# First transfers issued ahead of a branch, and one expert part's results added by matmuls instead of a store and a gather

## The chip, the core and the metric

The kernel runs on one core of a Trainium2 chip. The metric is the device time of one execution in microseconds (us); for the kernel before, the median of three runs is 1523.92 us, the lowest 1513.31 and the highest 1536.73. The core has engines that each work through an own queue in order: PE (TensorE, matmuls; its weight loads are listed apart as PEld), DVE (VectorE), ACT (ScalarE), POOL (GpSimd) and SP (SyncE, which here only issues transfers). Sixteen DMA engines carry the transfers that SP and POOL issue. Matmul results land in PSUM, everything else works in SBUF.

## The reference

The input x is 16 sequences of 256 tokens with 128 channels, 4096 tokens in all. Six sublayers follow each other, all with a residual:

```python
x = x + 0.5 * L0_ffn(layernorm(x))
x = x + L0_attn(layernorm(x))
x = x + 0.5 * L0_ffn(layernorm(x))
x = x + 0.5 * L1_ffn(layernorm(x))
x = x + L1_attn(layernorm(x))
x = x + 0.5 * L1_ffn(layernorm(x))
```

The attentions have 16 heads of 8 channels (layer 0 is the difference of two softmaxes, then a layernorm; layer 1 is causal with an output projection). Each feed-forward (FFN) is a mixture of eight experts of which each token uses two. For layer 1:

```python
gate_probs = softmax(xt @ Wg + bg)
top_v, top_i = top_k(gate_probs, 2)
w = top_v / (sum(top_v) + 1e-6)
a, g = split(xt @ W1[e] + b1[e]); act = a * gelu(g)
out = sum over the two experts of w * (act @ W2[e] + b2[e])
```

So a token's result is a weighted sum of two rows, one from each of its two experts. Layer 0 is alike with SwiGLU, 128 hidden channels in place of 256, no renormalised weights and one shared expert that every token uses.

## The kernel before, in words

**Blocks and parts.** The 4096 tokens are eight blocks of 512; all eight stay in SBUF as `xs[0..7]`. The first FFN treats blocks 0 and 1 densely (`dense`: all nine experts on the block, each expert's hidden rows multiplied by that expert's gate weight). The gate weights of a dense block are transposed into `cwT`, stored to DRAM (`cwD`) and loaded back as eight broadcast tiles `cwb` (line 897), each needed by one multiply on DVE.

All other FFN work is sparse and cut in parts of two blocks (`Sparse`, 16 parts); the last part of the last FFN is split into two parts of one block each: index 14 (block 6) and index 15 (block 7). A part goes through these tasks:

- `dispatch`: layernorm, gate logits, top two, and for each token and each of its two choices j the row (`idx`) it gets in a list of slots that is sorted by expert, each expert padded to a multiple of 128; and the two weights `wgt`, already halved.
- `scatter`: one indirect DMA per chunk of 128 tokens and per choice writes the normalised rows to `slots_x` in DRAM. The slots were zeroed by `clear_slots`.
- `load_tiles` and `compute`: for each tile of 128 slots the expert's weights are loaded from `wcat` (all weights and biases of an expert side by side, prepared in DRAM by `gather_weights`), and the rows from `slots_x`. A part of two blocks has 23 tiles, a part of one block 15. Two tiles at a time are transposed, multiplied, activated and multiplied again; the result y plus bias is stored to `slots_y`.
- `combine` and `add_to_x`: when all tiles of the part are stored, one indirect DMA per chunk and choice gathers the rows back (16 for a part of two blocks, 8 for one), and DVE adds each, times its weight, to x. The block's x is then final, and in the last FFN it is stored to the output.

**Order.** Nothing is ordered by hand. All tasks are generators that ask for an engine (`Ask`); a planner (`Tasks.run`) keeps a clock for each engine (`Clocks`, `Timed`: modelled durations) and gives the turn to the request with the smallest planned start plus 0.0048 us per rank (`HASTE`). Ranks are numbers by hand (`FFN_RANK`, `ATT_RANK`). The order so found is written into the engines' queues and is fixed on the chip. The planner books a DMA with 0.45 us on SP and its bytes at 300 GB/s behind the bytes ahead (`bytes_free`); a bulk transfer asks with `after=max(0.0, clocks.bytes_free - 3.0)`, not before the queue of bytes is shorter than 3 us. The indirect DMAs also wait for a matmul that the planner sees 1 us ahead of them ("pace", line 975).

**Branch.** A short calculation (`bound`, line 676) decides whether the scores of the attentions can overflow. Its result is read into a register (line 1306), and everything after is planned twice, once for each side of a branch. What is added to the planner ahead of line 1305 is planned and issued ahead of the branch: the loads that the first dense block needs, dense block 0, the normalised rows of blocks 0 and 1, and `bound`. `program` (line 1611) adds the rest, on each side: the clears, `gather_weights`, `dense(1)`, `loads(1)` (small constants and `xs[2..7]`), all sparse parts and attentions.

**Buffers** that the change touches: `big`, three PSUM tiles of 128x1024 (an FFN tile pair takes one for its hidden rows, an attention unit two); `b_s`, four SBUF tiles of 128x512; `b_y`, three; `b_cw`, two pairs of gate weight tiles for the dense blocks.

Of the kernel before, what the change touches and what calls it, by code (L numbers as in the profile page):

```python
# [9 lines left out]
FP = mybir.dt.float32  # L10
# [8 lines left out]
P = 128  # L19
# [10 lines left out]
HASTE = 0.0048  # L30

FFN_RANK = [
    [28, 13, 59],
    [190, 217, 235, 244],
    [218, 230, 258, 302],
    [450, 460, 412, 513, 477],
]
ATT_RANK = [
    [70, 127, 102, 103, 126, 127, 221, 222],
    [261, 262, 308, 271, 338, 301, 220, 513],  # L40
]


# [210 lines left out]
def kernel(ctx: ExitStack, tc: tile.TileContext, a: dict, out: bass.AP):  # L254
# [81 lines left out]
    def tile_of(shape, name, dtype=FP):  # L336
        return sb.tile(shape, dtype, name=name)
# [30 lines left out]
    )  # L368
    b_xn = buffers(5, [P, NCH, C], "xn")
    b_xnT = buffers(5, [P, TB], "xnT")  # L370
    b_cw = Buffers([(tile_of([P, NCH, E + 1], f"cw{i}"), tile_of([E + 1, TB], f"cwT{i}")) for i in range(2)])
    b_spread = buffers(3, [P, TB], "cwb")
    b_s = buffers(4, [P, TB], "s")
    b_h = buffers(3, [P, TB], "h")
# [114 lines left out]
    def loads(part):  # L489

        early = []
        for n in ("wq1", "wk1", "wq2", "wk2"):
            early.append((heads[n], a["L0_attn_" + n].rearrange("h c d -> c h d")))
        early += [(w1s[n], a["L1_attn_" + n]) for n in ("Wq", "Wk", "Wv")]
        early.append((heads["wv"], a["L0_attn_wv"].rearrange("h c d -> c h d")))
        early += [(xs[n], x_flat[n]) for n in range(2, PB)]
        late = [
            (sb2, a["L0_ffn_sb2"][0].partition_broadcast(P)),
            (gamma, a["L0_attn_ln_gamma"].partition_broadcast(P)),
            (beta, a["L0_attn_ln_beta"].partition_broadcast(P)),  # L500
            (lamb, a["L0_attn_lamb"].partition_broadcast(P)),
            (gate_w[1], a["L1_ffn_Wg"]),
            (gate_b[1], a["L1_ffn_bg"].partition_broadcast(P)),
            (w1s["Wo"], a["L1_attn_Wo"]),
            (b1_1raw, a["L1_ffn_b1"].rearrange("e (k f) -> (e k) f", f=P)),
        ]
        late += [(xs[n], x_flat[n]) for n in range(max(2, PB), NBLK)]
        for dst, src in early if part == 0 else late:
            yield Ask("SP")
            fetch(dst, src)  # L510

    def derived(part):
        if part == 0:
            yield from hidden_bias(b1_raw, b1_0)

            yield Ask("DVE", when=lambda: clocks.missing(b1_0) == 1)
            b = b1_0.rearrange("p (e k) -> p k e", k=2)[:, 0]
            nc.vector.tensor_scalar(b, b, 0.5, None, ALU.mult)
            return
        yield Ask("DVE", after=clocks.free["SP"] + 32.0)  # L520
        yield Ask("DVE", when=lambda: clocks.missing(sb2) == 1)
        nc.vector.tensor_scalar(sb2, sb2, 0.5, None, ALU.mult)

        yield Ask("DVE", after=clocks.free["SP"] + 60.0)
        yield vec(lamb, when=lambda: clocks.missing(gamma) == clocks.missing(beta) == 1)
        nc.vector.tensor_scalar(keep, lamb, -1.0, 1.0, ALU.mult, ALU.add)
        nc.vector.tensor_scalar(gamma, gamma, keep, None, ALU.mult)
        nc.vector.tensor_scalar(beta, beta, keep, None, ALU.mult)
        yield from hidden_bias(b1_1raw, b1_1)
# [10 lines left out]
    def clear_slots(h):  # L540
        v = slots_x[h].rearrange("(p i) d -> p i d", p=P)
        n = NSLOT // P
        step = -(-n // CLEAR)
        assert n > (CLEAR - 1) * step
        for i in range(0, n, step):
            m = min(step, n - i)
            yield Ask("SP", after=max(0.0, clocks.bytes_free - 3.0))
            nc.sync.dma_start(out=v[:, i : i + m, :], in_=zero.to_broadcast([P, m, C]))
# [10 lines left out]

    for layer in range(2):  # L560
        clocks.expect(wcat[layer], E // 4 + KF[layer] + 2)

    def gather_weights(layer, b1t, *deps):
        w1, w2, b2 = srcs[layer]
# [61 lines left out]
        number, pattern=[[1, NTILE], [0, E]], base=0, channel_multiplier=0,  # L626
        allow_small_or_imprecise_dtypes=True,
    )

    own4 = tile_of([P, 4, G], "own4")  # L630
    bare.gpsimd.memset(own4, 1.0)
# [239 lines left out]
    def dense_gates(run, rank):  # L871
        _, (tmp, gates, (cw, cwT)) = yield pe(
            run["xnT"], take=[(b_tmp, 1), (b_part, 1), (b_cw, 1)]
        )
        lg, taken = (t[:, :NCH] for t in gates)
        yield from gate_logits(run["xnT"], 0, lg)
        yield from choose(lg, taken)
        ex, mx = tmp[2][:, :NCH], tmp[6][:, :NCH].unsqueeze(2)
        yield from shares(lg, ex, mx)
        nc.vector.tensor_tensor(cw[:, :, 0:E], ex, taken, ALU.mult)  # L880
        nc.vector.memset(cw[:, :, E : E + 1], 1.0)
        b_tmp.put(tmp)
        b_part.put(gates)
        for i in range(BPB):
            _, (t,) = yield pe(cw, take=[(half, 1)])
            for c in range(NT):
                nc.tensor.transpose(t[: E + 1, c * P : (c + 1) * P], cw[:, i * NT + c, :], ident)
            yield from move(cwT[:, i * T : (i + 1) * T], t[: E + 1])
            half.put(t)
        run["cw"] = (cw, cwT)  # L890

        cwD = dram.tile([E + 1, TB], FP, name=f"cwD{run['n']}")
        yield Ask("SP", (cwT,))
        nc.sync.dma_start(out=cwD, in_=cwT)
        for e in range(E):
            _, (cwb,) = yield Ask("SP", (cwD,), take=[(b_spread, 1)])
            nc.sync.dma_start(out=cwb, in_=cwD[e : e + 1, :].to_broadcast([P, TB]))
            run["cwb"][e] = cwb

    def dense_expert(run, e):  # L900
# [31 lines left out]
            return  # L932
        nc.tensor.matmul(acc, lhsT=b2_0, rhs=run["cw"][1], start=False, stop=True)

        b_cw.put(run["cw"])
        b_xnT.put(xnT)
        _, (oT,) = yield Ask("ACT", (acc,), take=[(b_s, 1)])
        nc.scalar.copy(oT, acc)
# [41 lines left out]
    class Sparse:  # L980
        def __init__(self, index, layer, which, blocks, slots, rank, last=False):
            self.layer, self.last, self.rank = layer, last, rank
            self.after = 3 * layer + 2 * which
            self.blocks = blocks
            self.nch = len(blocks) * NCH
            self.ntile = 2 * self.nch + E - 1
            self.sx, self.sy = slots_x[slots], slots_y[slots]
            self.rows = rows_of[index]
            self.idx, self.wgt = (t[index][:, :, : self.nch] for t in (idx_of, wgt_of))
            self.gated = self.out_tiles = self.stored = 0  # L990
            self.scattered, self.weighed = [], False
            self.ready = False
            self.left = [NCH * 2 + (BPB if layer == 0 else 0) for _ in self.blocks]

        def add(self):
            tasks.add(self.rank - 5, self.dispatch())
            tasks.add(self.rank + 1, self.load_tiles())
            tasks.add(self.rank - 4, self.combine())

        def gate_block(self, i, xn, lg, taken):  # L1000
            n = self.blocks[i]
# [12 lines left out]
        def dispatch(self):  # L1014
# [96 lines left out]
            self.weighed = True  # L1111
            b_tmp.put(tmp)
            b_part.put(gates)

        def scatter(self, xns):
            def one(c, j):
                def issue(_):
                    row = xns[c // NCH][:, c % NCH, :]
                    s = bare.gpsimd.indirect_dma_start(  # L1119
                        out=self.sx[:, :],  # L1120
                        out_offset=bass.IndirectOffsetOnAxis(ap=self.idx[:, j, c : c + 1], axis=0),
                        in_=row, in_offset=None,
                    )
                    for t in self.scattered:
                        tc.declare_no_dep(s.ins, t.ins, reason="no slot twice")
                    self.scattered.append(s)
                    return s, [row, self.idx], self.sx

                return issue, (self.idx,)

            for i in range(len(xns)):
                todo = [one(c, j) for c in range(i * NCH, (i + 1) * NCH) for j in range(2)]
                yield from transfers(todo, lambda: not clocks.missing(self.sx))
                b_xn.put(xns[i])

        def shared(self, i, xnT):
            x = xs[self.blocks[i]]
# [67 lines left out]
        def compute(self, j, wts, xg, i0, last):  # L1205
# [53 lines left out]
                )  # L1259
            half.put(t)  # L1260
            b_wt.put(*wts)

            self.out_tiles += n
            late = 3.0 if self.out_tiles < self.ntile else 0.0
# [3 lines left out]
            )  # L1268
            b_y.put(y)
            self.stored += n  # L1270

        def combine(self):

# [22 lines left out]


    tasks.add(1, loads(0))
    tasks.add(0, derived(0))
    tasks.add(5, constants())  # L1300
    tasks.add(3, bound())
    for n in range(PB):
# [306 lines left out]
            bare.vector.tensor_copy(dst, m32.rearrange("p b t -> p (b t)"))  # L1609

    def program(shifted):
        for part in range(NPART):
            tasks.add(30 * (part + 3) % (30 * NPART), clear_slots(part))
        tasks.add(1, gather_weights(0, b1_0[:, 2 : 2 + 2 * E], b1_0))
        tasks.add(200, gather_weights(1, b1_1, b1_1))
        for n in range(1, PB):
            tasks.add(10 + n, dense(n, 10 + n))
        tasks.add(0, loads(1))
        tasks.add(3, derived(1))
        i = 0  # L1620
        for layer in range(2):
# [94 lines left out]
```

## Time and profile before

The profile is that of one execution, taken by the hardware profiler.

| what | value |
|---|---|
| median of three runs | 1523.92 us |
| the profiled execution | 1530.02 us |
| its span, first to last instruction | 1528.2 us |
| PE busy | 1244.2 us, 81% of the span |
| DVE busy | 933.3 us, 61% |
| ACT busy | 810.9 us, 53% |
| POOL busy | 621.2 us, 41% |
| mean granted PE clock | 0.904 of full speed |
| DMA | 232.87 MB, 152 GB/s on average |

How to read it: in the timeline a row is start, length, engine, source line, operation, tile written <- tile read, count; in brackets the idle time of the engine just before it, and what ended it. Nearly all instructions go through a helper at line 136, so the tile names tell them apart. "SPq" is SP's queue issuing a transfer; the data land later. The names are stripped of buffer numbers. The tiles `rw` and `cwb` are reused after the dense blocks: as `rw` also expert weights of sparse tiles are loaded, as `cwb` also rows of `slots_x`. A matmul of two 4-byte operands shows as two records.

### The profile page before, as it was taken

What the parts mean: (1) busy time and instruction counts of PE and PEld (TensorE: products, weight loads), DVE (VectorE), ACT (ScalarE), POOL (GpSimd) and SP (SyncE); (2) the same over time, 40 slices, a digit from 0 to 9 for tenths busy, and PEclk for the clock granted to TensorE, in tenths of its full rate; (3) what the DMA queues carried; (4) which work ended last, traced back from release to release, by engine and by line L of the source; (5) the groups of instructions that cost most, each with busy time, mean ns of one, the idle gap of its engine ahead of it and who ended that gap; (6) DMA issues with size and microseconds to landing.
All of it is one profiled execution on the core that took longest, in us unless ns stands there. A gap on an engine that the chain in (4) does not pass through costs nothing. (4 is left out here: it accounts for less than half of the span.)

```text
span 1528.2 us, 29302 instructions
## 1 busy us (share of the span) xinstructions
PE 1244.2 (81%) x9730; PEld 844.2 (55%) x9730; DVE 933.3 (61%) x3254; ACT 810.9 (53%) x1715; POOL 621.2 (41%) x629
## 2 busy tenths in 40 slices
PE   5848987888998988988987877788879789877872
PEld 3424554654444554545755665567468556656762
DVE  4464775855555545657666666878666664665543
ACT  2213555666776756656764564455546556653421
POOL 2013235344004044054264266653662564556233
PEclk8866999999999999899998999989789889988987
DMA  5185466651003435213756755565158542648893
GB/s 116 55 201 154 142 179 191 186 168 36 3 3 103 126 102 152 79 57 125 220 176 193 234 157 159 150 207 168 62 194 291 180 134 93 199 147 294 264 289 105
DMA packets 207531, 232.87 MB, mean 152 GB/s; under 512 B 32061, under 2 KB 151544, under 8 KB 207370
## 3 DMA queue, kind: packets, MB, share of 16 engines
q1 hardware_dynamic: 192010, 199.42, 42.9%
q0 software_dynamic: 15360, 31.49, 6.3%
q8 instruction: 79, 1.29, 0.4%
q14 instruction: 82, 0.67, 0.1%
HBM read 183.84 MB, written 52.75 MB: 155 GB/s over the span
## 5 line engine op out<-in xcount | busy, mean ns | idle before, releaser
L136 ACT ACTIVATE ex<-big 128x1024 f32<-128x1024 f32 (+1 forms) x384 | 350.2, 960 | 88.9 <-PE big L136 64.7
L1119 POOL DMA_INDIRECT slots_x<-xn,idx x240 | 242.0, 1008 | 270.3 <-PE big L136 86.9
L1278 POOL DMA_INDIRECT g<-slots_y,idx x240 | 236.4, 985 | 214.4 <-PE bank L136 94.9
L136 PE MATMUL big<-q,k 32*128 32x512 f32 (+1 forms) x1536 | 252.7, 639 | 14.6 <-ACT ex L136 5.8
L136 PE MATMUL big<-xT,wt 128*128 128x128 f32 x1456 | 222.4, 300 | 20.2 <-ACT xT L136 9.3
L136 PEld LDWEIGHTS big<-xT,wt 128*128 128x128 f32 x1456 | 203.1, 214 | 35.9 <-ACT xT L136 17.2
L136 PE MATMUL bank<-ex,vaug 128*32 128x256 f32 (+1 forms) x3072 | 189.4, 378 | 18.7 <-issue 6.3
L136 POOL TENSOR_TENSOR rstd<-rstd,mhalf 128x4 f32<-128x4 f32 (+1 forms) x64 | 62.1, 971 | 326.9 <-DVE rstd L136 325.8
L136 ACT ACTIVATE s<-big,wt 128x128 f32<-128x128 f32 x472 | 141.1, 377 | 87.9 <-PE big L136 54.4
L136 PEld LDWEIGHTS bank<-ex,vaug 128*32 128x32 f32 x3072 | 93.3, 113 | 92.0 <-issue 29.0
L136 PE MATMUL bank<-wt,h 128*128 128x128 f32 x728 | 118.6, 296 | 19.4 <-issue 7.8
L136 DVE SCALAR_TENSOR_TENSOR h<-big,wt,s 128x128 f32<-128x128 f32 x364 | 107.4, 343 | 41.4 <-ACT s L136 39.6
L136 PEld LDWEIGHTS big<-q,k 32*128 32x128 f32 x1536 | 82.6, 194 | 83.6 <-issue 50.0
L136 PEld LDWEIGHTS bank<-wt,h 128*128 128x128 f32 x728 | 99.5, 202 | 50.0 <-issue 20.2
L136 DVE SCALAR_TENSOR_TENSOR x<-g,wgt,x 128x128 f32<-128x128 f32 x240 | 88.5, 373 | 56.0 <-DMA g<-slots_y,idx 37.4
L136 PE MATMUL big<-xT,rw 128*128 128x128 f32 x716 | 113.2, 292 | 10.4 <-ACT s L136 3.7
L136 DVE TENSOR_TENSOR y<-bank,wt 128x128 f32<-128x128 f32 x236 | 59.8, 283 | 98.1 <-PE bank L136 34.3
L136 ACT COPY xT<-bank 128x256 f32<-128x256 f32 x180 | 61.4, 375 | 101.8 <-PE bank L136 63.2
L136 ACT COPY avs<-bank 128x256 f32<-128x256 f32 x96 | 36.1, 376 | 144.3 <-PE bank L136 71.8
L136 POOL TENSOR_TENSOR ex<-ex,causal 128x512 f32<-128x512 f32 x58 | 73.8, 1295 | 87.5 <-ACT ex L136 86.9
L136 PEld LDWEIGHTS big<-xT,rw 128*128 128x128 f32 x716 | 98.2, 204 | 19.1 <-issue 5.7
L136 ACT ACTIVATE s<-big,rw 128x128 f32<-128x128 f32 x232 | 72.1, 382 | 45.1 <-PE big L136 19.5
(192 smaller groups left out, 1835.2 us busy)
## 6 DMA issues: line engine op xcount, KB each, us to landing
wt<-wcat SPq DMA_DIRECT2D x128, 450.0 KB
rw<-wcat SPq DMA_DIRECT2D x63, 450.0 KB
wt<-wcat SPq DMA_DIRECT2D x108, 257.0 KB
slots_y<-y SPq DMA_DIRECT2D x168, 128.0 KB
rw<-wcat SPq DMA_DIRECT2D x53, 257.0 KB
cwb<-slots_x SPq DMA_DIRECT2D x45, 256.0 KB
xg<-slots_x SPq DMA_DIRECT2D x31, 256.0 KB
slots_x<-zero SPq DMA_DIRECT2D x12, 384.0 KB
```

Source lines behind the costliest of these rows:

```text
L136: r = f(*args, **kw)
L1119: s = bare.gpsimd.indirect_dma_start(out=self.sx[:, :], out_offset=bass.IndirectOffsetOnAxis(ap=self.idx[:, j, c : c + 1], axis=0), in_=ro ...
L1278: s = bare.gpsimd.indirect_dma_start(out=g[:, :], out_offset=None, in_=self.sy[:, :], in_offset=bass.IndirectOffsetOnAxis(ap=self.idx[:, j ...
```

## The change

Three things are changed.

1. *Ahead of the branch.* `loads(1)`, `gather_weights(0, ...)` and the clears of all four slot buffers are added to the planner ahead of line 1305 instead of in `program`. The loads of part 1 ask like other bulk transfers (`bytes_free - 3.0`). The two fixed delays in `derived(1)`: the first (32 us after SP's planned time) is 5 us.
2. *Part 14 is folded.* For this part, y is not stored and gathered. Each of its 8 pairs of chunk and choice writes for every token the pair (token number within the block, weight) to its slot in a small DRAM list `slots_t`, zeroed before; the list is loaded into SBUF as `told`, slot by partition. For each tile of 128 slots DVE builds a 128x512 matrix w (slot by token) that has the weight where the slot's token is, and zero elsewhere; four matmuls with w as the stationary operand add y's rows into an accumulator of 512 tokens in PSUM, held in one of the three `big` tiles from the first to the last tile of the part. Then one add on DVE brings it into x. The row of token numbers (`token`) takes the place of the gate weight tile of a dense block, so that tile has 128 partitions now.
3. *Ranks.* Ranks of some parts and attentions have other numbers.

The diff, cut:

```diff
 FFN_RANK = [
-    [28, 13, 59],
+    [33, 13, 59],
     [190, 217, 235, 244],
-    [218, 230, 258, 302],
-    [450, 460, 412, 513, 477],
+    [218, 230, 258, 222],
+    [450, 462, 417, 513, 466],
 ]
 ATT_RANK = [
-    [70, 127, 102, 103, 126, 127, 221, 222],
-    [261, 262, 308, 271, 338, 301, 220, 513],
+    [70, 125, 102, 103, 126, 127, 221, 222],
+    [261, 262, 295, 273, 340, 303, 270, 512],
 ]
...
         for dst, src in early if part == 0 else late:
-            yield Ask("SP")
+            yield Ask("SP", after=max(0.0, clocks.bytes_free - 3.0) if part else 0.0)
             fetch(dst, src)
...
-        yield Ask("DVE", after=clocks.free["SP"] + 32.0)
+        yield Ask("DVE", after=clocks.free["SP"] + 5.0)
...
+            self.fold = index == 14
+            self.acc, self.told, self.added = None, [], 0
...
+            if self.fold:
+                tasks.add(-10, clear_told())
+                self.left = [1]
+            else:
+                tasks.add(self.rank - 4, self.combine())
...
+            if self.fold:
+                nc.vector.tensor_copy(telling[:, :, :, 1], wgt)
+                yield from self.tell()
...
+        def tell(self):
+            yield Ask("POOL", writes=(token,))
+            nc.gpsimd.iota(token, pattern=[[1, TB]], base=0, channel_multiplier=0, ...)
...
+                    s = bare.gpsimd.indirect_dma_start(
+                        out=slots_t[:, :],
+                        out_offset=bass.IndirectOffsetOnAxis(ap=self.idx[:, j, c : c + 1], axis=0),
+                        in_=telling[:, j, c, :], in_offset=None,
+                    )
...
+            yield from transfers([one(c, j) for c in range(NCH) for j in range(2)])
+            yield Ask("SP", (slots_t,))
+            ld = nc.sync.dma_start(out=told, in_=slots_t.rearrange("(i p) k -> p i k", p=P))
...
+            if self.fold:
+                yield from self.fold_in(j, n, y)
+                return
...
+        def fold_in(self, j, n, y):
+            for i in range(n):
+                _, (w,) = yield Ask(
+                    "DVE", (told,), take=[(b_s, 1)], when=lambda: len(self.told) == 2 * NCH
+                )
+                nc.vector.tensor_scalar(
+                    w, token, told[:, j + i, 0:1], told[:, j + i, 1:2], ALU.is_equal, ALU.mult
+                )
...
+                acc = self.acc[:, 0, :]
+                yield pe(w, y, writes=[acc])
+                for c in range(NCH):
+                    nc.tensor.matmul(
+                        acc[:, c * P : (c + 1) * P], lhsT=w[:, c * P : (c + 1) * P],
+                        rhs=y[:, i, :], start=(self.added == c == 0),
+                        stop=(self.added == self.ntile - 1 and c == NCH - 1),
+                    )
+                self.added += 1
+                b_s.put(w)
+            b_y.put(y)
+            if self.added == self.ntile:
+                x = xs[self.blocks[0]].rearrange("p c d -> p (c d)")
+                yield vec(acc)
+                nc.vector.tensor_tensor(x, acc, x, ALU.add)
+                big.put(self.acc)
+                self.part_done(0)
...
+    tasks.add(2, loads(1))
+    tasks.add(11, gather_weights(0, b1_0[:, 2 : 2 + 2 * E], b1_0))
+    for part in range(NPART):
+        tasks.add(12 + 30 * (part + 3) % (30 * NPART), clear_slots(part))
...
     def program(shifted):
-        for part in range(NPART):
-            tasks.add(30 * (part + 3) % (30 * NPART), clear_slots(part))
-        tasks.add(1, gather_weights(0, b1_0[:, 2 : 2 + 2 * E], b1_0))
         tasks.add(200, gather_weights(1, b1_1, b1_1))
         for n in range(1, PB):
             tasks.add(10 + n, dense(n, 10 + n))
-        tasks.add(0, loads(1))
         tasks.add(3, derived(1))
```

More of the change, by code (lines that the diff above doesn't have):

```diff
@@ L370 @@
     b_xnT = buffers(5, [P, TB], "xnT")
-    b_cw = Buffers([(tile_of([P, NCH, E + 1], f"cw{i}"), tile_of([E + 1, TB], f"cwT{i}")) for i in range(2)])
+    b_cw = Buffers([(tile_of([P, NCH, E + 1], f"cw{i}"), tile_of([P, TB], f"cwT{i}")) for i in range(2)])
+    token = b_cw.free[1][1]
     b_spread = buffers(3, [P, TB], "cwb")
@@ L561, with clear_told @@
         clocks.expect(wcat[layer], E // 4 + KF[layer] + 2)
+    def clear_told():
+        yield Ask("SP")
+        nc.sync.dma_start(
+            out=slots_t.rearrange("(p i) k -> p (i k)", p=P),
+            in_=zero[:, 0, : 2 * NTOLD],
+        )
     def gather_weights(layer, b1t, *deps):
@@ L628 @@
     )
+    telling = tile_of([P, 2, NCH, 2], "telling")
+    bare.gpsimd.iota(
+        telling[:, :, :, 0], pattern=[[0, 2], [P, NCH]], base=0, channel_multiplier=1,
+        allow_small_or_imprecise_dtypes=True,
+    )
+    NTOLD = 2 * NCH + E - 1
+    slots_t = dram.tile([NTOLD * P, 2], FP, name="slots_t")
+    told = tile_of([P, NTOLD, 2], "tile_told")
     own4 = tile_of([P, 4, G], "own4")
@@ L874, in dense_gates @@
         )
+        run["bufs"] = (cw, cwT)
+        cwT = cwT[: E + 1]
         lg, taken = (t[:, :NCH] for t in gates)
@@ L933, in dense_expert @@
         nc.tensor.matmul(acc, lhsT=b2_0, rhs=run["cw"][1], start=False, stop=True)
-        b_cw.put(run["cw"])
+        b_cw.put(run["bufs"])
         b_xnT.put(xnT)
@@ L997, in add @@
             tasks.add(self.rank + 1, self.load_tiles())
-            tasks.add(self.rank - 4, self.combine())
+            if self.fold:
[3 more added lines that the diff above has]
+                tasks.add(self.rank - 4, self.combine())
         def gate_block(self, i, xn, lg, taken):
@@ L1134, in scatter, with one, issue @@
                 b_xn.put(xns[i])
+        def tell(self):
+            yield Ask("POOL", writes=(token,))
+            nc.gpsimd.iota(
+                token, pattern=[[1, TB]], base=0, channel_multiplier=0,
+                allow_small_or_imprecise_dtypes=True,
+            )
+            def one(c, j):
+                def issue(_):
+                    s = bare.gpsimd.indirect_dma_start(
[3 more added lines that the diff above has]
+                    )
+                    for t in self.told:
+                        tc.declare_no_dep(s.ins, t.ins, reason="no slot twice")
+                    self.told.append(s)
+                    return s, [telling, self.idx], slots_t
+                return issue, (telling, self.idx)
+            yield from transfers([one(c, j) for c in range(NCH) for j in range(2)])
+            yield Ask("SP", (slots_t,))
+            ld = nc.sync.dma_start(out=told, in_=slots_t.rearrange("(i p) k -> p i k", p=P))
+            for s in self.told:
+                tc.add_manual_dep(ld.ins, s.ins.name, SYNC, reason="every slot may be here")
         def shared(self, i, xnT):
@@ L1270, in compute @@
             self.stored += n
+        def fold_in(self, j, n, y):
+            for i in range(n):
+                _, (w,) = yield Ask(
+                    "DVE", (told,), take=[(b_s, 1)], when=lambda: len(self.told) == 2 * NCH
+                )
+                nc.vector.tensor_scalar(
+                    w, token, told[:, j + i, 0:1], told[:, j + i, 1:2], ALU.is_equal, ALU.mult
+                )
+                if self.acc is None:
+                    yield pe(w, y, when=lambda: self.acc is not None or big.free)
+                if self.acc is None:
+                    self.acc = big.free.pop()
+                acc = self.acc[:, 0, :]
[5 more added lines that the diff above has]
+                        stop=(self.added == self.ntile - 1 and c == NCH - 1),
+                    )
+                self.added += 1
[7 more added lines that the diff above has]
+                self.part_done(0)
         def combine(self):
```

## The prediction

> **What bounds the kernel now.** First the page's slices of the span, to find where TensorE (PE) is not filled; a digit is a tenth of a slice of 38.2 us, PEclk the granted clock.
>
> ```profile
> PE   5848987888998988988987877788879789877872
> PEclk8866999999999999899998999989789889988987
> DMA  5185466651003435213756755565158542648893
> ```
>
> The middle is full of PE work. Two places are not: slices 3 and 4 (76 to 153 us: clock at 0.6, DMA at 0.8), and the end, where DMA is at 0.8 to 0.9 for four slices and the last slice has almost no PE. The view of busy time by stretches prices both; columns are length, then PE, PE weight loads, DVE, ACT, POOL busy, then clock, DMA share, GB/s.
>
> ```profile
> 50.00:60.00 10.00, 8.74 (x32) 4.72 (x31) 7.95 (x13) 4.58 (x9) 0.00 (x0) 1.00 0.09 26
> 69.00:140.00 71.00, 43.05 (x126) 23.62 (x126) 38.48 (x137) 16.10 (x32) 8.07 (x8) 0.58 0.69 188
> 90.00:100.00 10.00, 0.00 (x0) 0.00 (x0) 9.41 (x38) 1.49 (x3) 1.42 (x2) 0.50 1.01 219
> 140.00:165.00 25.00, 23.42 (x131) 10.80 (x132) 16.31 (x53) 12.49 (x20) 15.07 (x16) 1.00 0.56 162
> 1405.00:1504.00 99.00, 75.54 (x563) 70.85 (x561) 48.00 (x197) 34.73 (x113) 30.23 (x32) 0.90 0.84 265
> ```
>
> Before the branch (it falls at 68.9 us) DMA is idle; after it 71 us hold only 43.05 x 0.58 = 25 us of full-clock PE work. The timeline shows what waits there.
>
> ```profile
> 68.92 3.26 SPq L136 DMA_DIRECT2D slots_x<-zero  x4
> 77.58 5.20 SPq L136 DMA_DIRECT2D x<-in_L_attn_x_dram  x6
> 84.03 0.29 DVE L136 BATCH_NORM_STATS2 st<-x 128x6 f32<-128x128 f32 x1 [6.26 <-DMA x<-in_L_attn_x_dram]
> 93.33 5.37 SPq L136 DMA_DIRECT2D wcat<-b_0t  x1
> 100.69 0.69 PE L136 MATMUL bank<-ident,xn 128*128 128x128 f32 x2 [16.09 <-DVE q L136]
> 112.12 0.31 SPq L136 DMA_DIRECT2D cwD<-cwT  x1
> 132.00 0.69 DVE L136 TENSOR_TENSOR h<-h,cwb 128x512 f32<-128x512 f32 x1
> ```
>
> DVE, in order, stands 6.26 us at the statistics of an x block that is fetched late; its held-up work then keeps PE idle for 16.09 us, and the second dense block's weights (cwb) are multiplied in only at 132. Last, the end:
>
> ```profile
> 1500.46 0.95 POOL L1278 DMA_INDIRECT g<-slots_y,idx  x1 [28.24 <-PE bank L136]
> 1502.93 0.61 PE L136 MATMUL bank<-rw,h 128*128 128x128 f32 x4
> 1503.58 0.29 DVE L136 TENSOR_TENSOR y<-bank,rw 128x128 f32<-128x128 f32 x1
> 1512.72 10.36 SPq L136 DMA_DIRECT2D out_dram<-x  x2
> 1519.85 0.95 POOL L1278 DMA_INDIRECT g<-slots_y,idx  x1 [0.30 <-issue]
> 1522.33 0.35 DVE L136 SCALAR_TENSOR_TENSOR x<-g,wgt,x 128x128 f32<-128x128 f32 x1 [0.90 <-DMA g<-slots_y,idx]
> ```
>
> PE is done at 1503.5, and 24.7 us follow to the span's 1528.2: sixteen gathers, one per 1.25 us on POOL (0.95 and 0.30 of issue), eight for each of the two one-block parts, then the last add and a store of 5.5 us. The first part's eight adds end with the first output at 1512.72.
>
> [...] 0.50 granted around the 16 us gap, 1.00 once PE is filled. [...] the two gathers timed cleanly in the chain take 2.24 and 2.41 us. [...] the trace's copy of b1_0t, 8 KB in 2048 pieces, held SP 5.37 us.
>
> **Part 1, transfers ahead of the branch.** Moved are 35 SP issues: 14 loads (8 small ones, 6 x blocks of 256 KB), 5 of the layer-0 weight gather (2 MB), 16 clears (5.9 MB), 9.4 MB in all. After the branch they took SP and DMA from 68.9 to about 115. From 20 to 69 us DMA was busy 12, 41, 8, 9 and 1% by tens, so there are some 42 us of room. Worth of it: the 71 us stretch. By PE alone, filled as in 140 to 165 (0.94), its 25 us would take 27: a gain of 44, the upper end. By DVE, 38.48 us of work: at 0.65 as in that next stretch 59 us (gain 12), at 0.94 as in 90 to 100 us 41 us (gain 30), at the middle, 0.80, 48 us (gain 23). I take **25**, a little over the middle, since some of that DVE work can move behind the stretch. The rest of the kernel is a chain of PE-filled stages and moves up with it. What is late next is DVE, then the second block's cwb.
>
> The cost is ahead of the branch. SP's queue is moved past by the cwD store and eight cwb loads of the first dense block (issued 28.0 to 51.8); the planner lets 3 us of bytes stand ahead of a bulk transfer, so a cwb can come 3 to 10 us late, the upper end with the 5.37 us of the b1_0t copy. Behind cwb wait DVE's multiply, then all behind it on DVE, then PE; the branch waits for them. DVE had a wait of 10.7 us at 44.9, where some of it hides. I take **+3**, range 0 to 10. No POOL instruction moves; POOL's first scatter (134.1) waits for clears that now end earlier.
>
> **Part 2, the fold of part 14.** Removed: 8 stores of y (15 tiles of 64 KB, 0.96 MB: 3.6 us at 265 GB/s), 8 gathers (10 us of POOL), 8 DVE adds (0.373 each, 3.0). Added on DVE: 15 weight builds 128x512, for which no row stands; 0.38 (the two-scalar row at 128x128) to 0.75 (the 128x512 row), taken 0.7: 10.5 us, hidden as DVE is at 48% from 1405 on, and as the weights can be built ahead of y. On PE: 4 matmuls a tile, recorded as 8 of about 0.112 us (16 took 1.79): 0.9 a tile, 13.4 in all, where PE is busy 75.5 of 99 us and DMA (0.84) sets the pace: most go into the 23 idle us. If that cover is gone, all 13.4 are on the path; none if DMA stays the bound; I take **+3**. On POOL: an iota (about 1 us by the 128x64 and 128x184 rows, 0.23 and 0.43) and 8 little scatters at 1.25: 11 us, beside a queue that idled 28 us before the end; the other part's gathers could slip by that. On SP: a clear and a load of 1920 pieces of 8 bytes, 0.5 to 5 us once, against 3.6 us of store issues saved: zero. DMA is relieved by 3.6; taken **-3**.
>
> The tail: last y at 1503.87, fold 1.1, add of acc to x 0.75, waits 0.3, store 5.5: 1511.5, that is -16.7. The other part's eight gathers, if still begun at 1500.46, end the kernel at 1512.7 + 5.5 = 1518.2: -10. With its rank lowered from 477 to 466 its tiles come a little sooner; I take **-14**.
>
> **Part 3, the ranks.** A rank counts 0.0048 us of planned start, so 80 ranks are 0.4 us: they reorder, not shift. Zero, with 8 us either way for another order. The shorter waits of the derived constants: zero.
>
> **Sum** against the profiled execution (1530.0; span 1528.2 and 1.8 around it): -25 +3 +3 -3 -14 = -36, so 1494. That execution stands 6.1 over the median of the runs shown (1523.9), so for the median 1488, 2.4% less.
>
> **Rivals.**
> *The lead is given back.* The stretch after the branch could be a latency chain (gate, choose, cwT, cwD, cwb), and the lead could run into a later stage that DMA sets. For it: from 100 to 120 us PE answers ACT and DVE piece by piece. Against: DVE's 6.26 us stand at a transfer, and the middle is PE-filled with DMA at 0 to 0.5 from slice 10 to 17. Front gain 5, tail 10: about 1509.
> *Slower, by PSUM.* The accumulator holds one of the three big tiles from its first fold to the end. From 1405 to 1504 there are 46 y adds, some 27 pairs of tiles, one per 3.7 us; with two tiles left, a pair may hold its tile 7.4 us. The trace shows 4.5 (1476.84 to 1481.35), but 10.8 in a stall (1453.54 to 1464.3). At 12 us held a pair takes 6: 27 x 2.3 = +62; less a tail of 14 and a front of 13 makes +35, 1559. It decides from about 11.5 us held.
> *It does nothing.* The moved transfers stand in SP's queue behind cwb loads that wait for DVE, and are issued at 50 to 69 us, little sooner than now; the fold's gathers are replaced by the other part's. About 1522.
>
> **Numbers.** Main case 0.80, its own range 1466 (DVE at 0.94, -30; no cost ahead; tail -17, relief -3; run scatter of 10) to 1503 (gain 12, cost 3, tail -10 and +3, -3; less scatter); 0.68 of it lies over 2% below the median (under 1493.4). Given back 0.06, nothing 0.03, slower 0.11. A change of about 2% is what a measurement of this kernel can tell from none. Faster 0.68, same 0.21, slower 0.11; the range 1464 to 1518 leaves out the slower case and a little at each end.
>
> **What would show it.** Right: x loads issued before the branch; no DVE wait for x; PE busy over 55 of the first 71 us after the branch at a clock over 0.8; the branch within 72 us; at the end eight gathers under the last matmuls and 8 to 15 us from the last matmul to the end. Wrong: DVE waiting for cwb before the branch for over 10 us; idle PE gaps after it that end with DVE as now; after 1400, PE waiting for a big tile to be freed, or a last stage longer by the whole 13 us.

## The result, and the profile after

The changed kernel takes 1504.44 us at the median of 10 runs (1493.35 to 1509.55), the kernel before 1522.66 of 10 on the same chip: a ratio of 0.988, 95% interval [0.9853, 0.9908], so 18.2 us or 1.2% less. The profiled execution took 1503.24 us (span 1501.5) against 1530.02; that pair differs by 26.8, since the profiled run of before was a long one. Four of the runs further down lie over 1.5% above the fastest of their kernel: the medians as given include them, the ratios and the differences between kernels in us leave them out.

The slices of the span of the changed kernel (37.5 us each):

```profile
PE   5768888899999898988987878778788888887886
PEclk8678999999999999899998999999998999989889
DMA  7545566730002443213656655455566255648974
```

The third slice of PE is 6 in place of 4, and the last 6 in place of 2; DMA is now at work in the second. But the second slice has a clock of 6, before 8, and PE of 7, before 8. The timelines show why. First of the kernel before:

```profile
26.54 0.30 SPq L136 DMA_DIRECT2D cwD<-cwT  x1
...
28.02 23.79 SPq L136 DMA_DIRECT2D cwb<-cwD  x8
...
32.33 1.89 DVE L136 TENSOR_TENSOR h<-h,cwb 128x512 f32<-128x512 f32 x3
...
58.96 0.69 DVE L136 TENSOR_TENSOR h<-h,cwb 128x512 f32<-128x512 f32 x1
...
68.08 0.16 DVE L136 TENSOR_SCALAR bounded<-bank 128x1 int32<-128x1 f32 x1 [0.68 <-PE bank L136]
```

Then of the changed kernel (`bounded` is the result of `bound`):

```profile
22.73 4.57 SPq L136 DMA_DIRECT2D x<-in_L_attn_x_dram  x5
27.41 0.36 SPq L136 DMA_DIRECT2D cwD<-cwT  x1
...
29.02 3.94 SPq L136 DMA_DIRECT2D slots_x<-zero  x3
...
34.67 1.54 SPq L136 DMA_DIRECT2D cwb<-cwD  x3
...
49.26 0.29 DVE L136 TENSOR_TENSOR ex<-bank,ident 128x128 f32<-128x128 f32 x1 [17.97 <-PE bank L136]
...
55.19 0.16 DVE L136 TENSOR_SCALAR bounded<-bank 128x1 int32<-128x1 f32 x1 [0.68 <-PE bank L136]
55.26 1.88 DVE L136 TENSOR_TENSOR h<-h,cwb 128x512 f32<-128x512 f32 x3
55.97 1.52 SPq L136 DMA_DIRECT2D cwb<-cwD  x3
...
69.06 11.95 SPq L136 DMA_DIRECT2D slots_x<-zero  x10
...
76.12 0.69 DVE L136 TENSOR_TENSOR h<-h,cwb 128x512 f32<-128x512 f32 x1
...
108.93 0.66 PE L136 MATMUL bank<-ident,xn 128*128 128x128 f32 x2 [4.78 <-DVE xn L136]
...
120.67 0.68 DVE L136 TENSOR_TENSOR h<-h,cwb 128x512 f32<-128x512 f32 x1
```

The x loads stand at 22.73, far ahead of the branch. But between the store of cwD and the first cwb loads other transfers are issued, three clears among them, and the cwb loads leave at 34.67 in place of 28.02.

The trace also keeps the time and size of each DMA packet, and the store of cwD and the cwb loads are the only transfers of that time in packets of 2048 bytes, so their ends can be read. The last packet of the first three cwb loads ended at 32.5 us before and at 42.3 us in the changed kernel, 9.8 us later: SP issued the first of the three 6.6 us later, and from there to the end of the third it was 7.7 us in place of 4.5.

DVE's first three multiplies by cwb come at 55.26 (before: 32.33), 22.9 us later, and so 13 us after those three loads had ended. DVE did not wait for a transfer there: it idled 17.97 us for PE's chain of `bound`, which its queue now has ahead of those multiplies. Before, the multiplies came first, and the result of `bound` only at 68.08. The branch falls at 82 us, not 69. Behind it DVE waits for no x load any more, and the second dense block reaches its first multiply at 120.67, not 132.00. Busy time by stretches of the changed kernel (columns as in the prediction):

```profile
40.00:50.00 10.00, 7.14 (x24) 5.37 (x24) 0.29 (x1) 1.86 (x5) 0.00 (x0) 0.50 0.66 151
50.00:60.00 10.00, 7.20 (x17) 4.31 (x17) 3.88 (x12) 0.00 (x0) 0.00 (x0) 0.50 0.26 80
...
100.00:110.00 10.00, 2.83 (x14) 1.47 (x14) 9.38 (x45) 1.19 (x4) 3.13 (x3) 0.59 0.38 116
...
82.00:153.00 71.00, 54.71 (x160) 28.09 (x160) 57.55 (x192) 22.14 (x44) 25.68 (x24) 0.76 0.40 114
```

From 40 to 55 us PE works through one dependent chain, that of `bound`, at half clock (0.50, and so up to 60), with DVE busy 0.29 us from 40 to 50 and 3.88 from 50 to 60. The 71 us behind the branch now hold 54.71 x 0.76 = 42 us of full-clock PE work, before 25. From 100 to 110 DVE is full and PE waits for it. The end of the changed kernel, from the timeline:

```profile
1482.38 0.95 POOL L1369 DMA_INDIRECT g<-slots_y,idx  x1 [33.84 <-DVE h L136]
...
1486.58 3.81 PE L136 MATMUL big<-y,s 128*128 128x128 f32 x32 [0.23 <-issue]
...
1491.31 0.69 DVE L136 TENSOR_TENSOR x<-big,x 128x512 f32<-128x512 f32 x1 [2.13 <-PE big L136]
...
1492.03 4.66 SPq L136 DMA_DIRECT2D out_dram<-x  x2
1492.53 0.94 POOL L1369 DMA_INDIRECT g<-slots_y,idx  x1 [0.30 <-issue]
...
1495.93 0.35 DVE L136 SCALAR_TENSOR_TENSOR x<-g,wgt,x 128x128 f32<-128x128 f32 x1 [0.59 <-DMA g<-slots_y,idx]
```

Eight gathers are left, under the last matmuls; the folded part is added at 1491.31, and the other part's last gather ends the kernel. From the last matmul (1490.4) to the end of the span are 11.1 us, before 24.7.

To see where time is won along the way, the table gives when PE had finished a share of its matmul work other than the fold's (each matmul record weighted by a fixed cost of its shape; so it compares equal work):

| share of PE's work | before, us | after, us | after is ahead by |
|---|---|---|---|
| 4% | 83.0 | 96.8 | -13.8 |
| 5% | 137.8 | 129.2 | 8.6 |
| 20% | 349.2 | 335.3 | 13.9 |
| 70% | 1056.1 | 1044.3 | 11.8 |
| 80% | 1204.4 | 1180.9 | 23.5 |
| 100% | 1503.5 | 1485.5 | 18.0 |

13.8 us are lost ahead of the branch, 27.7 won behind it up to 20% of PE's work (22.4 of them between 4 and 5%), and a further 12 between 70 and 80%, where the front and the fold do nothing. The row at 5% lies inside a steep stretch and depends on the weights: with multiply-adds as weights it reads 130.6 and 127.5, while the leads of the other rows move by 1.1 us at most.

### The profile page after: what moved, and what is told of

Same layout as the page of the kernel before. It is cut to its first block, busy times and chain, and to the rows that moved or that the text cites. A ratio compares the mean times of both kernels' runs of the same rounds, so it can differ in the third digit from the quotient of the medians.

```text
span 1501.5 us, 29536 instructions
## 1 busy us (share of the span) xinstructions
PE 1253.5 (83%) x9850; PEld 856.8 (57%) x9850; DVE 950.7 (63%) x3268; ACT 801.8 (53%) x1711; POOL 610.1 (41%) x622
## 5 line engine op out<-in xcount | busy, mean ns | idle before, releaser
L1369 POOL DMA_INDIRECT g<-slots_y,idx x232 | 229.6, 990 | 217.3 <-PE bank L136 47.4
L136 PE MATMUL big<-q,k 32*128 32x512 f32 (+1 forms) x1536 | 249.1, 631 | 10.0 <-DVE h L136 3.9
L136 PE MATMUL big<-xT,wt 128*128 128x128 f32 x1456 | 216.7, 294 | 18.1 <-issue 5.0
L136 PEld LDWEIGHTS big<-xT,wt 128*128 128x128 f32 x1456 | 196.3, 208 | 31.3 <-issue 9.9
L136 PEld LDWEIGHTS big<-xT,rw 128*128 128x128 f32 x716 | 102.3, 211 | 11.0 <-ACT xT L136 4.5
L136 DVE COPY oall<-bank 128x144 f32<-128x144 f32 x96 | 28.9, 302 | 99.1 <-PE bank L136 79.1
```

Source lines behind the costliest of these rows:

```text
L136: r = f(*args, **kw)
L1369: s = bare.gpsimd.indirect_dma_start(out=g[:, :], out_offset=None, in_=self.sy[:, :], in_offset=bass.IndirectOffsetOnAxis(ap=self.idx[:, j ...
```

## The experiments

The theory after the first traces: the front gains 22 us and costs 13, not 3, since bulk bytes ahead of cwD and cwb led the planner to put `bound` first; the fold gains its tail. The rivals: re-ordering (ranks) makes the difference; the fold's matmuls lie on the path. The three groups of runs below come from three chips. On the first one the kernel before takes 1425.94 us, on the others 1535.17 and 1524.26, so times are compared on one chip only, and ratios (to the kernel before on the same chip) across chips.

**The parts, one by one.** The front alone (`e1_front`): the changed kernel with the old ranks and

```diff
-            self.fold = index == 14
+            self.fold = False
```

> Only the transfers ahead of the branch; the last part stored and gathered as before, ranks as before. My theory (the transfers gain about 22 us after the branch and cost about 13 ahead of it; the fold gains 14 at the end): branch near 82 us as in the changed kernel, 7 to 12 us faster than before by the runs' medians, and some 24 us from the last matmul to the end as before. Rival, the re-ordering (new ranks and a new order of the planner's make the difference, the transfers nothing): within 4 us of before. Rival, the front brings it all: 18 us or more faster than before.

Measured: 1417.19 us, ratio 0.9941 [0.9921, 0.996], 8.8 us less at the medians. The fold alone (`e2_fold`): the changed kernel with the old ranks, and `loads(1)`, `gather_weights(0, ...)`, the clears and the 32 us delay put back into their places of before.

> Only the fold of the one-block part; transfers behind the branch and ranks as before. My theory: branch at 69 us, about 10 us from the last matmul to the end, 8 to 14 us faster than before. Rival, the fold's 13 us of matmuls fall on the path of the end stage: tail shorter by 14 but the kernel within 4 us of before. Rival, re-ordering: anything, and not the sum of its parts with the run of the front alone.

Measured: 1421.67 us, ratio 0.9986 [0.9966, 1.0007]: 2 us by the ratio, 4.3 by the medians. Both together with the old ranks (`e3_old_ranks`: only the two tables of ranks put back):

> The changed kernel with the ranks of before: front and fold together. My theory (a rank shifts a planned start by 0.0048 us, so ranks only re-order): within 8 us of the changed kernel, and the gains of the front alone and of the fold alone add up in it within 5 us. Rival, the ranks are what makes the change faster: 1518 us or more, near before.

Measured: 1413.74 us, ratio 0.9927 [0.9901, 0.9954]. The parts add up: 0.59% and 0.14% give 0.73%. And the new ranks alone (`e4_ranks`: the kernel before with the two new tables):

> The kernel before with the new ranks alone. My theory: within 8 us of before, either sign. Rival, the ranks make the difference: 12 us or more faster than before.

Measured: 1480.62 us, ratio 1.0421 [1.0363, 1.048]: **slower by 4%**. Neither theory had that. The timeline of this kernel has one stall that the others lack:

```profile
1062.25 0.96 POOL L1119 DMA_INDIRECT slots_x<-xn,idx  x1 [0.30 <-issue]
...
1067.75 1.09 PE L136 MATMUL bank<-ident,cwb 128*128 128x128 f32 x4 [20.51 <-DMA cwb<-slots_x]
```

In the new order PE's queue has a tile at its head whose rows are still being scattered: POOL issues 30 scatters from 1014 to 1062 us, one per 1.27 us for most of them, and PE stands 20.51 us. So a few ranks of 0.0048 us each can place a wait of 20 us. (More of the 55 us is lost step by step after it: against `e2_fold`, run on the same chip, it is level at 60% of PE's work, 31 us behind at 80% and 55 at 94%.)

The front's own term is read best from `e3_old_ranks` beside `e2_fold` on one chip, which differ in the front alone: at 4% of PE's work the former is 12.4 us behind (95.7 and 83.3), at 5% 9.8 ahead (128.3 and 138.1), at 50% 11.6, at 100% 8.4. The lead made behind the branch is carried to the end. The fold's term is small although its tail is there, as the timelines show, of `e1_front`:

```profile
1388.92 0.95 POOL L1369 DMA_INDIRECT g<-slots_y,idx  x1 [25.74 <-PE bank L136]
...
1391.39 0.61 PE L136 MATMUL bank<-rw,h 128*128 128x128 f32 x4
...
1410.95 0.35 DVE L136 SCALAR_TENSOR_TENSOR x<-g,wgt,x 128x128 f32<-128x128 f32 x1 [0.90 <-DMA g<-slots_y,idx]
```

and of `e3_old_ranks`:

```profile
1392.20 0.94 POOL L1369 DMA_INDIRECT g<-slots_y,idx  x1 [32.88 <-DVE h L136]
...
1395.95 4.75 PE L136 MATMUL big<-y,s 128*128 128x128 f32 x40 [0.67 <-DVE s L136]
...
1406.41 0.35 DVE L136 SCALAR_TENSOR_TENSOR x<-g,wgt,x 128x128 f32<-128x128 f32 x1 [3.51 <-DMA g<-slots_y,idx]
```

From the last matmul to the end it is 24.9 us and then 11.3. But the last matmul is now one of the fold's: 40 of its 120 records come after all other PE work, which ends at 1395.3. From the end of that other work to the end of the span it is 24.9 us and then 16.7, so 8.2 us are won there, and not 13.6; the other part's eight gathers still set the end. And the last 7% of the other PE work take 105.5 us without the fold and 113.4 with it: nearly all of the 8.2 us is paid in the stage ahead.

**The whole change, and its front mended.** The changed kernel (`c1_after`), the kernel before (`c2_before`), and two variants of the changed kernel, on one chip.

> The changed kernel again, beside its parts on one chip. In the first four runs the front alone gave 0.6%, the fold alone 0.1%, both together 0.7%, and the new ranks alone cost 4%. If ranks only re-order and the order they make is a matter of what else has moved: ratio to before 0.985 to 0.990 here as well, 4 to 12 us better than with the old ranks. If the new ranks are bad in themselves: slower than with the old ranks, ratio above 1.0.

Measured: 1520.11 us of 4 runs, ratio 0.9826 [0.9742, 0.991].

> The kernel before, for a trace of it from the same chip: branch near 69 us, some 24 us from the last matmul to the end, as in the first trace; with the new ranks' stall of 20 us for rows of the slots near 1050 us absent.

Measured: 1532.89 us in one run, 24.8 us from the last matmul to the end; its DMA and PE slices repeat those of the first trace within a digit or two. Without the fold (`e4b_no_fold`, the diff of the first experiment, with the new ranks):

> The changed kernel without the fold: front and new ranks. If the fold is worth its tail (14 us) less 3 on PE: 8 to 14 us slower than the changed kernel. If it is worth little, as with the old ranks (2 us): within 5 us of it.

Measured: 1521.93 us of 4 runs, ratio 0.9887 [0.9825, 0.9949]: the fold is worth 6.5 us by the medians and 0.6%, or 9 us, by the ratios, whose intervals overlap widely. The two traces agree: from the end of the other PE work to the end of the span it is 25.0 us without the fold and 16.5 with it, and here the last 7% of that work take equally long in both, within 0.3 us. So with the new ranks the fold is worth some 6 to 9 us, as far as so few runs can tell. Then the guard (`e5_guard`), which holds the bulk transfers back until the third cwb load is issued:

```diff
+    bulk = []
...
-            yield Ask("SP", after=max(0.0, clocks.bytes_free - 3.0) if part else 0.0)
+            yield Ask("SP", when=lambda: bulk or not part, after=...)
...
-            yield Ask("SP", after=max(0.0, clocks.bytes_free - 3.0))
+            yield Ask("SP", when=lambda: bulk, after=max(0.0, clocks.bytes_free - 3.0))
...
             run["cwb"][e] = cwb
+            if e == 2:
+                bulk.append(1)
```

> The changed kernel, but no bulk transfer ahead of the branch is issued until the first dense block's third cwb load is. My theory (the 13 us ahead of the branch come from the byte queue in front of cwD and the first cwb, which made the planner put the multiplies by cwb behind the chain of bound): first multiply by cwb near 33 us in place of 55, branch at 69 to 74 us in place of 82, the second dense block no later than in the changed kernel minus 5 us, and 6 to 13 us faster than the changed kernel in the first 150 us. Rival (the branch is late because SP has more to issue ahead of it, or because DVE is short): branch still at 79 us or later. Rival (lead is given back): branch early, but the expert tiles begin no sooner and the time is within 4 us of the changed kernel.

Measured: 1553.45 us, ratio **1.0089** [1.0046, 1.0133]. What was expected ahead of the branch came: first multiply by cwb at 32.4 us, the result of `bound` at 67.3, and at 5% of PE's work 6.7 us ahead of `c1_after` (123.2 and 129.9). But the time is 38 us longer than that kernel's. The lead is 6.7 at 20%, -6.7 at 50%, 0.4 at 85%, and -24.5 at 100%: lost in stages that the guard doesn't touch. Either a lead is given back as a rule, or the planner, which reached the branch with other clocks, found another and worse order behind it.

**Order held.** To tell these apart, the guarded kernel got the planner's clocks of the changed kernel at the branch (`e9_guard_same_order`):

```diff
+    clocks.__dict__.update(copy.deepcopy(AT_BRANCH))
+    clocks.table = AF.Exp
     clocks.pe = []
     saved = copy.deepcopy(clocks.__dict__)
```

AT_BRANCH holds the numbers of the changed kernel. The planner decides by them alone. In the traces the instructions behind the branch stand in the changed kernel's order on every engine, and those ahead of it in the order of `e5_guard`. On the same chip: the changed kernel, one without most of the fold's matmuls, and the old ranks.

> The changed kernel, as the base for the next three on one chip: ratio to before 0.98 to 0.99.

Measured: 1502.55 us, ratio 0.9846 [0.9808, 0.9884].

> The guard again (no bulk transfer ahead of the branch until the first dense block's third cwb load is issued), but every engine's order behind the branch is held to that of the changed kernel, instruction by instruction; only what is ahead of the branch differs. My theory (the guard saves the 13 us ahead of the branch, and the earlier run with it was slower only because the planner, from another state, found a worse order behind it): branch at 69 to 73 us, lead over the changed kernel 8 to 14 us at a twentieth of PE's work and still 6 to 14 us at the end; 6 to 14 us faster than the changed kernel. Rival (lead ahead of the branch is always given back later): within 3 us of the changed kernel. Rival (the guard itself does harm, by late clears or late weights): slower than the changed kernel.

Measured: **1488.59 us, ratio 0.9737** [0.9696, 0.9779]: 15.9 us less than the changed kernel, 2.6% less than the kernel before. From its timeline:

```profile
27.21 1.27 SPq L138 DMA_DIRECT2D cwb<-cwD  x3
...
31.68 1.88 DVE L138 TENSOR_TENSOR h<-h,cwb 128x512 f32<-128x512 f32 x3
33.27 3.85 SPq L138 DMA_DIRECT2D x<-in_L_attn_x_dram  x5
...
59.13 0.68 DVE L138 TENSOR_TENSOR h<-h,cwb 128x512 f32<-128x512 f32 x1
66.42 0.16 DVE L138 TENSOR_SCALAR bounded<-bank 128x1 int32<-128x1 f32 x1 [0.78 <-PE bank L138]
...
105.21 0.68 DVE L138 TENSOR_TENSOR h<-h,cwb 128x512 f32<-128x512 f32 x1
```

The first cwb loads leave ahead of the x loads, the dense block runs as it did before the change, the bulk transfers fill what was idle (DMA's share by tens from 30 to 70 us is 0.69, 1.03, 1.12 and 0.93; before the change 0.41, 0.08, 0.09 and 0.01), and from the last multiply of the first block to the first one of the second it is 46.1 us (44.6 in the changed kernel; before, from 58.96 to 132.00, it was 73.0). Against `c3_after` it is 15.8 us ahead at 4% of PE's work, 16.2 at 5%, 13.1 at 50% and 13.4 at 100%. So the lead ahead of the branch is kept nearly in full where the order behind it stays. And the same guard with the planner's free choice behind it had a ratio of 1.0089 on another chip: **order alone moves this kernel by 3.5%** (0.9737 and 1.0089).

The fold with 13 of 15 tiles' matmuls left out, so that its results are incomplete (`e10_two_folds`):

```diff
-                for c in range(NCH):
-                    nc.tensor.matmul(
+                for c in range(NCH):
+                    args = acc[:, c * P : (c + 1) * P], w[:, c * P : (c + 1) * P], y[:, i, :]
+                    if 0 < self.added < self.ntile - 1:
+                        nc.tensor.book("matmul", args[0], args[1:], (), {})
+                        continue
+                    nc.tensor.matmul(
```

> The changed kernel with the fold's matmuls of 13 of the 15 tiles left out (the first and the last are kept; so the folded part's results are not all added), all else in the same order. That takes 52 of 60 matmuls, some 11.6 us, from PE in the last 100 us. Theory (the fold's matmuls lie on the path of the end stage, which is why the shorter tail brings only 2 to 4 us): 6 to 11 us faster than the changed kernel. Rival, as I had predicted (most go into PE's idle time): within 3 us.

Measured: 1502.58 us, ratio 0.9843 [0.9808, 0.9878], the same as the changed kernel's. The busy time of the end stage, of `c3_after`:

```profile
1405.00:1480.00 75.00, 61.40 (x474) 58.23 (x475) 36.25 (x136) 24.82 (x80) 24.62 (x26) 0.93 0.74 244
```

and of `e10_two_folds`:

```profile
1405.00:1480.00 75.00, 58.24 (x430) 54.87 (x428) 37.94 (x145) 26.47 (x85) 25.13 (x26) 0.91 0.76 244
```

PE has fewer matmuls and is idle for as much longer: its busy time is 3.2 us shorter in the same 75 us. Of the 6 to 11 us that the matmuls would cost if they lay on the path nothing is seen in the medians, and from the last 7% of the other PE work to the end under 2 us in the two traces. The ratios alone would not exclude 6 us (0.4% on each, so some 8 us on their difference). It is also the order in which the fold did not lengthen the stage. What makes the stage 8 us longer with the old ranks is open: the order that the planner finds there, one `big` tile fewer, or PE after all, since the matmuls were left out in the other order alone.

The old ranks again (`c4_old_ranks`, the same kernel as `e3_old_ranks`):

> The changed kernel with the ranks of before again, beside the changed kernel on one chip. If the new ranks are worth what the ratios of different chips say (0.9826 and 0.988 against 0.9927): 7 to 15 us slower than the changed kernel. If that was the difference of the chips: within 4 us.

Measured: 1518.33 us, ratio 0.9957 [0.9936, 0.9977]: with the old ranks 15.2 us slower than `c3_after`. At 70% of PE's work the new ranks are 6.6 us ahead, at 80% 19.2, at 100% 12.9. So the gain between 70 and 80% in the first pair of traces is theirs.

## Why the prediction was right, and where not

The direction and the range held: 1504 in 1464 to 1518. The forecast was a gain of 36 us and half of that came, and from other parts than the sum said.

- **The front behind the branch, -25.** Right: -27.7 from 4 to 20% of PE's work, -22.4 of it up to 5% (the stretch from the first block's last multiply by cwb to the second's first is 28.5 shorter). DVE's wait for x is gone, DVE is what is late next (9.38 of 10 us from 100 on), and the lead is carried on, as `e3_old_ranks` beside `e2_fold` shows. PE was busy 54.71 of 71 us at 0.76, where over 55 at over 0.8 was asked. The rival "the lead is given back" fell.
- **The cost ahead of the branch, +3, range 0 to 10.** This step failed: it is 13 to 16 (13.8 in the first traces, 15.8 by `e9_guard_same_order`). The prediction had a cwb that lands 3 to 10 us late and DVE waiting for it. The first half came, at its upper end: the first three cwb loads ended 9.8 us late. The second did not: the planner booked the late bytes too, and answered by putting the chain of `bound` ahead of the multiplies on DVE; so DVE waited 17.97 us for PE, which ran that chain at half clock (0.50), and multiplied 13 us after the loads had ended; the branch fell at 82 us, where within 72 was asked. That a cwb comes late with bulk in front was the author's estimate. Measured with bulk in front, the store of cwD took 3.0 us from its issue to its last packet in place of 1.1, and the three cwb loads 7.7 in place of 4.5; the larger part of the 9.8 us, 6.6, is their later issue. How DMA shares its time between them was not shown. The "upper end with the 5.37 us of the b1_0t copy" did not come: that copy stood behind the first six cwb loads and took 0.43 us; and it is 1024 packets of 8 bytes in the traces, not 2048 pieces. What the rival "it does nothing" said of SP also came in part: the cwb loads of 55.97 waited for DVE, and 13 of the 16 clears stood behind them in SP's queue, at no visible cost.
- **The fold's PE work, +3.** Not seen: nothing by the medians of `e10_two_folds`, under 2 us by its trace; but 3 us is within what its intervals leave open (some 8 us), so the term is neither confirmed nor refuted.
- **The tail, -14.** Sized too high. From the last matmul to the end it is as forecast (24.7 to 11.1, -13.6), but from the end of the other PE work it is 24.7 to 16.1, -8.6, because the eight gathers of the other part still begin 3.1 us ahead of that end and set the end of the kernel. The prediction had worked out -10 for just this case, and took 4 more for an earlier start of that part, which did not come. With the old ranks the stage ahead of the tail also became 8 us longer, and the fold as a whole is worth 2 to 4 us there; with the new ranks 6 to 9. The rival "slower, by PSUM" fell in its size; whether the missing big tile has a share in these 8 us was not tried.
- **Relief of DMA, -3.** Not seen: DMA's share from 1405 us to the last matmul fell from 0.84 to 0.70, but the stage didn't get shorter by it.
- **The ranks, 0 with 8 either way.** This failed as well: -15.2 us in the changed kernel, +4.2% in the kernel before. "They reorder, not shift" is true, but a re-ordering has no small size: it can place a stall of 20 us (20.51 in `e4_ranks`).

With the terms as measured one after the other, front -8.5 (0.6%), fold with the old ranks -2, new ranks on top -15: -25.5, against gains of 1.2, 1.7 and 1.5% in three measurements (0.988, 0.9826, 0.9846), which are 18 to 27 us. The front was forecast too large by 13.5 and the fold by 12; the ranks, taken at nothing, gave back 15, perhaps in part because the fold is worth more with them. So the number stayed inside the range partly by luck, through errors of opposite sign.

## What to carry to other kernels

Work moved to where an engine or DMA seemed idle was not free here: ask which urgent small transfer it now stands in front of, and hold the bulk back until that one is issued (here a guard of a few lines was worth 15.9 us, once the order behind it was held). Where a planner writes the order, a change must be measured with the order behind it held, or the effect of re-ordering (here 3.5%, and 4.2% for the ranks alone) is taken for its own; and ranks tuned for one version need not suit another. A shorter tail counts only if the stage ahead of it ends no later, and it is counted from the end of the same work in both kernels.

## What the runs showed of the hardware

- The kernel before took 1425.9 us on one chip (that of `e1_front` to `e4_ranks`) and 1523 to 1535 on the others. Single DVE operations last the same (the `h` products from `big`, `wt` and `s` 343 ns on average, in `e2_fold` there and in `before`); over the runs of the kernel before, PE's mean granted clock is 0.923 to 0.939 on that chip and 0.897 to 0.916 on the others.
- The copy to `wcat` in 1024 pieces of 8 bytes held SP's queue for 5.37 us before the change, with a DMA share of 1.01 from 90 to 100 us, and for 0.43 us after it, with 0.26 from 50 to 60 us (0.74 during the copy); in `e9_guard_same_order`, with 1.12 from 50 to 60 us, for 4.57. So it went fast in the run with the low share and slowly in the two with a share over 1; what holds SP was not tried.
- Of three cwb loads on SP's queue, the last packet ended 4.5 us after the first was issued where nothing stood ahead of them (`before`), and 7.7 us where x loads, clears and weight copies did (`after`). With the guard (`e9_guard_same_order`) DVE's first multiply by cwb came 4.5 us after the first of them was issued (27.21 to 31.68), before the change 4.3 (28.02 to 32.33).
- In the changed kernel PE, up to 55 us in pieces of 0.56 to 1.23 us of one dependent chain, was busy 7.14 and 7.20 us from 40 to 50 and from 50 to 60, at a clock of 0.50 in both. From 70 to 80 it was busy 7.20 us as well, at a clock of 1.00.
